# Layer 1's self-attention in a two-layer decoder: layernorms and output in halves, projections three units later, a copy written as a maximum, first shifts placed ahead of two maxima

## The chip, the cores and the metric

The kernel runs on one core of one Trainium2 chip. The metric is the device time of one execution in microseconds (us). A core has five engines that run side by side and meet through semaphores: TensorE (PE in the profile; its weight loads are PEld), VectorE (DVE), ScalarE (ACT), GpSimd (POOL) and SyncE (SP), which here only issues DMAs. Each engine takes its own instructions in order. PE writes its results to PSUM, from where VectorE or ScalarE fetch them; PSUM is handed out in banks of 128 partitions by 512 fp32 values.

## The reference, cut to what matters

Two decoder layers, each self-attention, cross-attention and a feed-forward part, with a residual sum and a layernorm behind each. `x` is 2 batches of 1024 tokens with 256 features. The change lies in the second layer's self-attention (16 heads of 16 features) and in the two layernorms around it: the one behind layer 0's feed-forward part and its own.

```python
def _layernorm(x, axis=-1, eps=1e-05):
    m = jnp.mean(x, axis=axis, keepdims=True)
    v = jnp.var(x, axis=axis, keepdims=True)
    return (x - m) / jnp.sqrt(v + eps)

def _L1_attn_ref(x, W_qkv, b_qkv, W_proj, b_proj):
    B, N, C = x.shape
    qkv = (x @ W_qkv + b_qkv).reshape(B, N, 3, NUM_HEADS, HEAD_DIM)
    q, k, v = jnp.transpose(qkv, (2, 0, 3, 1, 4))
    scores = jnp.einsum('bhqd,bhkd->bhqk', q, k) * SCALE
    attn = jax.nn.softmax(scores, axis=-1)
    out = jnp.einsum('bhqk,bhkd->bhqd', attn, v)
    out = jnp.transpose(out, (0, 2, 1, 3)).reshape(B, N, C)
    return out @ W_proj + b_proj
...
x = _layernorm(x + _L0_ffn_ref(x, ...), axis=-1)
x = _layernorm(x + _L1_attn_ref(x, L1_attn_W_qkv, ...), axis=-1)
```

## The kernel before

The 2048 tokens are four groups (`g`) of 512: groups 0 and 1 are batch 0, groups 2 and 3 batch 1. A group's activations are a tile `x[g]` of 128 partitions by 4 tiles of 256 features.

`l1_attn` (from L1098) works through 16 **steps** `n`: batch, four heads (a quad) and half of the query rows. A step has eight **units**, one for each 128 keys (`kt`), so unit `u` belongs to step `u // 8`, and the loop runs over 128 units. Of PE, VectorE and ScalarE the order of instructions is the order of this Python text (`manual_schedule`); POOL and SP are ordered by a scheduler. In each unit stand, in this order:

- every eighth unit (7, 15, 23, ...), `shifts(n)` for the next step: four small VectorE operations on 128x16 values. L1197 takes the minimum of two halves, L1199 rounds it to the fp32r format, L1200 copies it into the tile `cz`, and L1201 writes what the rounding left off. They turn the softmax's row maxima into rows that a matmul can add to the scores;
- `maxima` twice: each time two matmuls (L1177), each into a bank of its own, and two VectorE reductions (L1187) that take the row maxima out of those banks. They run nine units ahead of the scores that need them. The banks come from a pool of three (`ps_t`), which the projections, transposes and outputs share;
- between the two, `products`: eight matmuls for the scores (L1222) and for adding the shift (L1228), and two exponentials on ScalarE (L1234);
- in the shift units `shifted(n)`: PE transposes `cz` (L1208), and VectorE brings the result to SBUF as `c` (L70);
- `mix` of the unit before: probabilities times values into the accumulator (L1248);
- `others(unit)`: what a table `extra` holds for this unit. `at(unit, f, ...)` fills the table.

That table carries all the rest. `project` makes queries and keys of a batch: PE (L1086), a bias on ScalarE (L1091), the upper bits on VectorE (L1094), the remainder on POOL (L1095: `ql` and `kl`). `stacks` copies them by DMA on SP into `qst` and `kst`, the layout that the matmuls read. `values` makes the values (L1134, L1139). `taken` and `quotient` divide a finished step by its sums (L1268, L1272, L1273). For a group whose heads are all done, `turned` transposes the attention's result (L1286), `output` multiplies it by the output weights (L1301) and adds it to a residual sum `r` (L1306), `weigh` takes the layernorm's statistics, `normed` scales, and `onward` transposes the new `x` for the next stage (L157). The layernorms of groups 2 and 3 from layer 0 also lie in the table, at units 11 and 19; those of groups 0 and 1 were done before the loop.

`moments` (L170 to L184) takes four `bn_stats` and four `bn_aggr` in turn (L178, L179), adds epsilon (L181) and lets POOL raise to the power -0.5 (L183); `scaled` then makes four scalings on VectorE (L200). The residual sum `r` starts as `x` plus the bias on POOL (L1294) in one of four buffers `r`. For groups 0 and 1 this buffer is the one that held the sums of groups 2 and 3, so the addition waits until L200 has read those.

Ahead of the loop, nine early units (-9 to -1) fill the maxima of step 0 and the first two of step 1 (L1182, 128x1024 at a time), with the values and projections of batch 0 in between; then come `shifts(0)` and `shifted(0)`. What group 3 needs at the end (`self.ends`) is interleaved with the first four iterations of the cross-attention.

The table's entries before:

```python
for g, unit in ((2, 11), (3, 19)):
    for k, f in enumerate((weigh, normed, self.turned)):
        at(unit + k, f, g)
...
at(first - 26 + i, project, b, quad // 2, name, blk)
...
at(first - 20 + 2 * k + i, stacks, b, 2 * quad + k, name)
...
at(first - 22 + k, values, b, k)
...
for k, f in ((10, turned), (11, output), (13, normed), (15, onward)):
    at(first + k, f, g)
```

`first` is `8 * n`. In the loop, projections are made for step 8 (`first` = 64) and step 12 (`first` = 96), so at units 38 to 41 and 70 to 73.

Of the kernel before, what the change touches and what calls it, by code (L numbers as in the profile page):

```python
# [9 lines left out]
F32 = mybir.dt.float32  # L10
# [5 lines left out]
ALU = mybir.AluOpType  # L16
# [17 lines left out]
class Decoder:  # L34
# [136 lines left out]
    def moments(self, r, tiles):  # L171

        nc = self.nc
        n = len(tiles)
        mv = self.sm.tile([P, 4, 2], F32, tag="mv", name="mv")
        for k, i in enumerate(tiles):
            st = self.sm.tile([P, 6], F32, tag="st", name="st")
            nc.vector.bn_stats(st, r[:, i, :])  # L178
# [5 lines left out]
        return mv, rstd  # L184

    def scaled(self, x, r, tiles, mv, rstd, by=None):
        nc = self.nc
# [909 lines left out]
    def l1_attn(self):  # L1097
# [3 lines left out]
        with ExitStack() as s:  # L1101
# [60 lines left out]
            def maxima(u, early=False):  # L1162

                if u >= 16 * len(steps):
                    return
                n, k = u // 16, u % 16 // 8
                qt, kb = divmod(u % 8, 2)
                b, quad, qb = steps[n]
                jp = 2 * quad + k
                if u % 16 == 0:  # L1170
                    most[n] = self.sm.tile([P, 2, 4, 4], F32, tag="most", name="most")
                q0 = qb * 512 + qt * P
                both = self.wide() if early else None
                sc = [both[:, a, :] if early else self.bank() for a in range(2)]
                for a in range(2):
                    rows = slice(64 * a, 64 * a + 64)
                    nc.tensor.matmul(  # L1177
                        sc[a], lhsT=stack[b, jp, "q"][rows, q0 : q0 + P],
                        rhs=stack[b, jp, "k"][rows, kb * 512 : (kb + 1) * 512], start=True, stop=True,
                    )  # L1180
                if early:
                    nc.vector.tensor_reduce(  # L1182
                        most[n][:, kb, qt, k : k + 3 : 2], both, AX.X, ALU.max, negate=True
                    )
                for a in range(0 if early else 2):
                    h = 2 * a + k
                    nc.vector.tensor_reduce(  # L1187
                        most[n][:, kb, qt, h : h + 1], sc[a], AX.X, ALU.max, negate=True
                    )

            def shifts(n):

                if n >= len(steps):
                    return
                cz = zeros[n % 2]
                nm = self.sm.tile([P, 4, 4], F32, tag="nm8", name="nm8")
                nc.vector.tensor_tensor(nm, most[n][:, 0], most[n][:, 1], ALU.min)  # L1197
                hi = self.sm.tile([P, 4, 4], F32R, tag="nmh", name="nmh")
                nc.vector.tensor_copy(hi, nm)  # L1199
                nc.vector.tensor_copy(cz[:, :, :, 0], hi.bitcast(F32))  # L1200
                nc.vector.tensor_tensor(cz[:, :, :, 1], nm, hi.bitcast(F32), ALU.subtract)  # L1201

            def shifted(n):
# [88 lines left out]
            def output(g):  # L1292
                r = self.rp.tile([P, 4, D], F32, tag="r", name="r")
                nc.gpsimd.tensor_tensor(  # L1294
                    r, self.x[g], self.lbp.unsqueeze(1).to_broadcast([P, 4, D]), ALU.add
                )
                for i in range(0, 4, 2):
                    ps = self.bank().rearrange("p (i d) -> p i d", i=2)
                    for k in range(2):
                        for c in range(2):  # L1300
                            nc.tensor.matmul(  # L1301
                                ps[:, k, :], lhsT=aT[g][:, c, (i + k) * P : (i + k + 1) * P],
                                rhs=wo[:, c, :], start=c == 0, stop=c == 1,
                            )
                    rv = r[:, i : i + 2, :]
                    nc.vector.tensor_tensor(rv, ps, rv, ALU.add)  # L1306
                weigh(g, r)

            sums = {}

            def weigh(g, r=None):
                r = self.sums[g] if r is None else r
                sums[g] = r, self.moments(r, range(4))

            def normed(g):
                r, moments = sums.pop(g)
                self.x[g] = self.xp.tile([P, 4, D], F32, tag="x", name="xg")
                self.scaled(self.x[g], r, range(4), *moments)

            def onward(g):  # L1320
                nxT[g] = self.transposed(self.x[g])
# [4 lines left out]
            def at(unit, f, *args):  # L1326
                extra.setdefault(unit, []).append((f, args))

            for g, unit in ((2, 11), (3, 19)):
                for k, f in enumerate((weigh, normed, self.turned)):  # L1330
                    at(unit + k, f, g)
            last = 8 * len(steps)
            both = [(name, blk) for name in "qk" for blk in range(2)]
            for n, (b, quad, qb) in enumerate(steps):
                first = 8 * n
                if qb == 0:
                    for i, (name, blk) in enumerate(both):
                        if quad % 2 == 0 and n > 4:
                            at(first - 26 + i, project, b, quad // 2, name, blk)
                    for i, name in enumerate("qk" if n else ()):  # L1340
                        for k in range(2):
                            at(first - 20 + 2 * k + i, stacks, b, 2 * quad + k, name)
                    if quad == 0 and n:
                        for k in range(4):
                            at(first - 22 + k, values, b, k)
                at(first + 8, taken, n)
                at(first + 9, quotient, n)
                if quad == 3 and n < len(steps) - 1:
                    g = 2 * b + qb
                    for k, f in ((10, turned), (11, output), (13, normed), (15, onward)):  # L1350
                        at(first + k, f, g)

            def others(unit):
                for f, args in extra.pop(unit, ()):
# [498 lines left out]
```

## Time and profile before

| what | us |
|---|---|
| median of 3 runs (2458.32 to 2465.51) | 2461.87 |
| the profiled execution | 2461.69 |
| its span, first to last instruction | 2459.9 |
| PE busy (14062 matmul records) | 2345.8 |
| VectorE busy | 1680.9 |
| ScalarE busy | 1106.2 |
| POOL busy | 910.4 |
| row maxima L1187 in layer 1's self-attention, 476 instructions, 683 ns each | 296.3 |
| first early maximum to last product of layer 1's self-attention | 1770.7 to 2241 |

The page divides the span into 40 slices of 61.5 us. Each digit is the busy share of a slice in tenths, PEclk the granted TensorE clock:

```profile
PE   7999999999998999999999999999999999999974
...
DVE  6887887888785234555555555555689687995776
...
PEclk9999999999999999999999999999989999999986
```

The digits from the 30th to the 37th slice are layer 1's self-attention: PE is at nine tenths or more, VectorE mostly at 6 to 9. The clock dips in the 30th slice.

In the stage itself the waits show in full only when single instructions are read in order of time; the trace gives each one's start, its length, and how long its engine idled before it, with the instruction that released it.

### The profile page before, as it was taken

What the parts mean: (1) busy time and instruction counts of PE and PEld (TensorE: products, weight loads), DVE (VectorE), ACT (ScalarE), POOL (GpSimd) and SP (SyncE); (2) the same over time, 40 slices, a digit from 0 to 9 for tenths busy, and PEclk for the clock granted to TensorE, in tenths of its full rate; (3) what the DMA queues carried; (4) which work ended last, traced back from release to release, by engine and by line L of the source; (5) the groups of instructions that cost most, each with busy time, mean ns of one, the idle gap of its engine ahead of it and who ended that gap; (6) DMA issues with size and microseconds to landing.
All of it is one profiled execution on the core that took longest, in us unless ns stands there. A gap on an engine that the chain in (4) does not pass through costs nothing.

```text
span 2459.9 us, 37289 instructions
## 1 busy us (share of the span) xinstructions
PE 2345.8 (95%) x14062; PEld 1599.9 (65%) x14065; DVE 1680.9 (68%) x2924; ACT 1106.2 (45%) x1722; POOL 910.4 (37%) x748
## 2 busy tenths in 40 slices
PE   7999999999998999999999999999999999999974
PEld 3545545545545668899999999999844444555742
DVE  6887887888785234555555555555689687995776
ACT  5665565565563322333333233333256554664344
POOL 4666566566565222342242433332210001002412
PEclk9999999999999999999999999999989999999986
DMA  7888788688787001010010010100212122210001
GB/s 158 174 159 168 149 169 169 131 163 171 148 172 187 1 0 41 1 39 27 13 35 25 23 35 12 48 1 1 47 28 40 30 37 34 44 27 1 1 1 35
DMA packets 275667, 168.78 MB, mean 69 GB/s; under 512 B 47560, under 2 KB 262176, under 8 KB 275488
## 3 DMA queue, kind: packets, MB, share of 16 engines
q1 hardware_dynamic: 239072, 148.05, 28.8%
q10 hardware_dynamic: 36416, 18.36, 3.7%
q8 instruction: 111, 1.82, 0.3%
q14 instruction: 68, 0.56, 0.1%
HBM read 34.21 MB, written 2.10 MB: 15 GB/s over the span
## 4 chain that ended last, share of the span: by engine, by line
PE 73%; DVE 12%; DMA 4%; SPq 3%; issue 3%; ACT 3%; POOL 1%; ACTq 0%; DVEq 0%; POOLq 0%
PE unit L917 16%; PE acc L965 9%; PE bank L965 7%; PE wide L297 6%; PE acc L1248 5%; PE acc L379 4%; PE bank L1177 3%; SPq L358 3%; PE bank L252 3%; DMA turned<-blocks 3%; PE wide L649 2%; DVE most L1187 2%; PE bank L662 2%; DVE blocks L342 2%; PE wide L1222 2%
## 5 line engine op out<-in xcount | busy, mean ns | idle before, releaser
L312 DVE TENSOR_REDUCE nm<-wide 128x1 f32<-128x1024 f32 x256 | 300.9, 1215 | 62.9 <-PE wide L297 61.9
L1187 DVE TENSOR_REDUCE most<-bank 128x1 f32<-128x512 f32 x476 | 296.3, 683 | 23.7 <-PE bank L1177 23.3
L1234 ACT ACTIVATE w<-wide 128x1024 f32<-128x1024 f32 x256 | 248.2, 1022 | 140.9 <-PE wide L1228 132.0
L297 PE MATMUL wide<-k,q 64*128 64x512 f32 x1024 | 274.0, 632 | 18.0 <-ACT p L317 16.6
L328 POOL TENSOR_SCALAR p<-p,sums 128x1024 f32<-128x1024 f32 x128 | 143.1, 1118 | 270.6 <-DVE sums L325 270.6
L379 PE MATMUL acc<-turned,v 128*64 128x256 f32 x2048 | 235.1, 382 | 2.2 <-ACT aoT L74 1.3
L379 PEld LDWEIGHTS acc<-turned,v 128*64 128x64 f32 x2048 | 142.6, 137 | 114.3 <-issue 34.8
L906 ACT ACTIVATE mhT<-mhT,cols 128x256 f32<-128x256 f32 (+1 forms) x256 | 143.3, 607 | 147.4 <-DVE mhT L934 104.9
L317 ACT ACTIVATE p<-wide,nm 128x1024 f32<-128x1024 f32 x128 | 142.8, 1116 | 144.9 <-DVE nm L312 118.6
L817 POOL TENSOR_TENSOR hs<-hs,mhT 128x1024 f32<-128x1024 f32 x31 | 102.4, 3305 | 241.8 <-DVE hs L815 241.8
L342 DVE STREAM_TRANSPOSE blocks<-p 128x1024 f32<-128x1024 f32 x128 | 158.1, 1235 | 45.9 <-DMA turned<-blocks 19.8
L297 PEld LDWEIGHTS wide<-k,q 64*128 64x128 f32 x1024 | 90.4, 187 | 145.3 <-issue 74.5
L917 PE MATMUL unit<-xT,w 128*128 128x256 f32 x768 | 182.2, 379 | 0.0
L183 POOL TENSOR_TENSOR rstd<-ve,nhalf 128x4 f32<-128x4 f32 (+2 forms) x28 | 26.1, 932 | 421.4 <-DVE ve L181 421.0
L974 DVE SCALAR_TENSOR_TENSOR r<-acc,gates,r 128x128 f32<-128x128 f32 x256 | 77.8, 346 | 140.0 <-PE acc L965 140.0
L342 DVE STREAM_TRANSPOSE blocks<-r 128x1024 f32<-128x1024 f32 x128 | 153.9, 1203 | 0.0
L1177 PE MATMUL bank<-kst,qst 64*128 64x512 f32 x476 | 139.1, 480 | 14.8 <-DVE most L1187 14.5
L917 PEld LDWEIGHTS unit<-xT,w 128*128 128x128 f32 x768 | 140.9, 190 | 16.9 <-issue 0.3
L1177 PEld LDWEIGHTS bank<-kst,qst 64*128 64x128 f32 x476 | 67.5, 188 | 127.1 <-DVE most L1187 105.1
L328 POOL TENSOR_SCALAR r<-r,sums 128x1024 f32<-128x1024 f32 x128 | 143.2, 1119 | 0.0
L317 ACT ACTIVATE r<-wide,nm 128x1024 f32<-128x1024 f32 x128 | 142.3, 1111 | 1.0 <-DVE nm L312 0.7
L1248 PE MATMUL acc<-w,v 128*32 128x512 f32 x1024 | 140.5, 621 | 0.0
(332 smaller groups left out, 4604.7 us busy)
## 6 DMA issues: line engine op xcount, KB each, us to landing
turned<-blocks SPq DMA_DIRECT2D x636, 128.0 KB, 2.8
turned<-blocks ACTq DMA_DIRECT2D x132, 128.0 KB, 3.2
w<-in_L_ffn_W SPq DMA_DIRECT2D x16, 1024.0 KB, 5.2
q<-q SPq DMA_DIRECT2D x64, 128.0 KB, 2.3
k<-k SPq DMA_DIRECT2D x32, 128.0 KB, 2.7
qst<-qh SPq DMA_DIRECT2D x48, 64.0 KB, 2.4
qst<-ql SPq DMA_DIRECT2D x48, 64.0 KB, 2.4
kst<-kh SPq DMA_DIRECT2D x48, 64.0 KB
```

What stands on the lines that cost most here:

```text
L297: nc.tensor.matmul(sc[h][:, kb, :], lhsT=q[rows, qi, at : at + P], rhs=k[rows, ki, :], start=True, stop=True,)
L312: nc.vector.tensor_reduce(nm, sc, AX.XY, ALU.max, negate=True)
L317: nc.scalar.activation(p, sc.rearrange("p a c -> p (a c)"), AF.Exp, bias=nm, accum_out=sums[:, 0, h : h + 1],)
L328: nc.gpsimd.tensor_scalar(p, p, sums[:, 1, h : h + 1], 1.0, ALU.mult, ALU.mult)
L342: nc.vector.transpose(blocks[m][:, :, h, qt, :], p.rearrange("p (j q) -> p j q", q=32))
L379: nc.tensor.matmul(av[own[h], 0:256].rearrange("p (t i q) -> p i t q", t=2, i=4), lhsT=vals[u][:, kt, own[h]], rhs=p[:, h], start=kt == 0, ...
L917: nc.tensor.matmul(v[:, m, :], lhsT=up[e][k][:, f : f + P], rhs=self.halves[g][k], start=k in (1, 2, 5) and m == 0, stop=True, skip_group_ ...
L965: nc.tensor.matmul(ps[at][:, m * P : (m + 1) * P], lhsT=h[k][:, c, m * P : (m + 1) * P], rhs=down[e][k][:, c, :], start=k in (1, 2, 5) and ...
L1177: nc.tensor.matmul(sc[a], lhsT=stack[b, jp, "q"][rows, q0 : q0 + P], rhs=stack[b, jp, "k"][rows, kb * 512 : (kb + 1) * 512], start=True, s ...
L1187: nc.vector.tensor_reduce(most[n][:, kb, qt, h : h + 1], sc[a], AX.X, ALU.max, negate=True)
L1234: nc.scalar.activation(slot[:, k, :], ps[k].rearrange("p a q -> p (a q)"), AF.Exp, scale=0.25)
L1248: nc.tensor.matmul(mixed[n][o : o + 32, :], lhsT=vals[b][:, kt, 17 * h : 17 * h + 32], rhs=pT[:, a, :], start=kt == 0, stop=kt == 7, tile_ ...
```

## The change

The layernorm gets a second form in halves. `weighed` takes the statistics of two tiles (two `bn_stats`, then two `bn_aggr`), with epsilon and the power behind the second half; `scaled_half` scales two tiles. `output` is split in two halves, with its residual addition on POOL in a function of its own, `residual`. The table is refilled accordingly, so that the pieces stand in units of their own and the chain of a group ends two units later. All of `project`, `stacks` and `values` move three units later. In `shifts` the second copy is written as a maximum over an axis of length one. `shifts(0)` moves ahead of the maxima of unit -1. A function `turned_half` is added that nothing calls (left out below).

```diff
--- before.py
+++ after.py
@@ -182,6 +182,37 @@
         rstd = self.sm.tile([P, 4], F32, tag="rstd", name="rstd")
         nc.gpsimd.tensor_tensor(rstd[:, 0:n], ve[:, 0:n], self.nhalf[:, 0:n], ALU.pow)
         return mv, rstd
+
+    def weighed(self, r, mv=None):
+
+        nc = self.nc
+        tiles = (0, 1) if mv is None else (2, 3)
+        if mv is None:
+            mv = self.sm.tile([P, 4, 2], F32, tag="mv", name="mv")
+        st = [self.sm.tile([P, 6], F32, tag="st", name="st") for _ in tiles]
+        for k, i in enumerate(tiles):
+            nc.vector.bn_stats(st[k], r[:, i, :])
+        for k, i in enumerate(tiles):
+            nc.vector.bn_aggr(mv[:, i, :], st[k])
+        if tiles[0] == 0:
+            return mv
+        ve = self.sm.tile([P, 4], F32, tag="ve", name="ve")
+        nc.vector.tensor_scalar(ve, mv[:, :, 1], EPS, None, ALU.add)
+        rstd = self.sm.tile([P, 4], F32, tag="rstd", name="rstd")
+        nc.gpsimd.tensor_tensor(rstd, ve, self.nhalf, ALU.pow)
+        return mv, rstd
+
+    def scaled_half(self, x, r, half, mv, rstd):
+        i = slice(2 * half, 2 * half + 2)
+        self.scaled(x, r, range(2 * half, 2 * half + 2), mv[:, i, :], rstd[:, i])
+
...
 
     def scaled(self, x, r, tiles, mv, rstd, by=None):
         nc = self.nc
@@ -1197,7 +1228,10 @@
                 nc.vector.tensor_tensor(nm, most[n][:, 0], most[n][:, 1], ALU.min)
                 hi = self.sm.tile([P, 4, 4], F32R, tag="nmh", name="nmh")
                 nc.vector.tensor_copy(hi, nm)
-                nc.vector.tensor_copy(cz[:, :, :, 0], hi.bitcast(F32))
+
+                nc.vector.tensor_reduce(
+                    cz[:, :, :, 0], hi.bitcast(F32).unsqueeze(3), AX.X, ALU.max
+                )
                 nc.vector.tensor_tensor(cz[:, :, :, 1], nm, hi.bitcast(F32), ALU.subtract)
 
             def shifted(n):
@@ -1289,33 +1323,42 @@
                         )
                     self.evac(aT[g][:, c, :], ps)
 
-            def output(g):
-                r = self.rp.tile([P, 4, D], F32, tag="r", name="r")
+            sums = {}
+
+            def residual(g):
+                r = sums[g] = self.rp.tile([P, 4, D], F32, tag="r", name="r")
                 nc.gpsimd.tensor_tensor(
                     r, self.x[g], self.lbp.unsqueeze(1).to_broadcast([P, 4, D]), ALU.add
                 )
-                for i in range(0, 4, 2):
-                    ps = self.bank().rearrange("p (i d) -> p i d", i=2)
-                    for k in range(2):
-                        for c in range(2):
-                            nc.tensor.matmul(
-                                ps[:, k, :], lhsT=aT[g][:, c, (i + k) * P : (i + k + 1) * P],
-                                rhs=wo[:, c, :], start=c == 0, stop=c == 1,
-                            )
-                    rv = r[:, i : i + 2, :]
-                    nc.vector.tensor_tensor(rv, ps, rv, ALU.add)
-                weigh(g, r)
-
-            sums = {}
-
-            def weigh(g, r=None):
-                r = self.sums[g] if r is None else r
-                sums[g] = r, self.moments(r, range(4))
-
-            def normed(g):
-                r, moments = sums.pop(g)
-                self.x[g] = self.xp.tile([P, 4, D], F32, tag="x", name="xg")
-                self.scaled(self.x[g], r, range(4), *moments)
+
+            def output(g, half):
+                ps = self.bank().rearrange("p (i d) -> p i d", i=2)
+                for k in range(2):
+                    for c in range(2):
+                        i = 2 * half + k
+                        nc.tensor.matmul(
+                            ps[:, k, :], lhsT=aT[g][:, c, i * P : (i + 1) * P],
+                            rhs=wo[:, c, :], start=c == 0, stop=c == 1,
+                        )
+                rv = sums[g][:, 2 * half : 2 * half + 2, :]
+                nc.vector.tensor_tensor(rv, ps, rv, ALU.add)
+
+            moments = {}
+
+            def weigh(g, half):
+                if half == 0:
+                    sums.setdefault(g, self.sums[g])
+                moments[g] = self.weighed(sums[g], moments.get(g))
+
+            def normed(g, half):
+                if half == 0:
+                    new[g] = self.xp.tile([P, 4, D], F32, tag="x", name="xg")
+                self.scaled_half(new[g], sums[g], half, *moments[g])
+                if half:
+                    self.x[g] = new.pop(g)
+                    del sums[g], moments[g]
+
+            new = {}
 
             def onward(g):
                 nxT[g] = self.transposed(self.x[g])
@@ -1327,8 +1370,10 @@
                 extra.setdefault(unit, []).append((f, args))
 
             for g, unit in ((2, 11), (3, 19)):
-                for k, f in enumerate((weigh, normed, self.turned)):
-                    at(unit + k, f, g)
+                for k, f in enumerate((weigh, normed)):
+                    for half in range(2):
+                        at(unit + 2 * k + half, f, g, half)
+                at(unit + 4, self.turned, g)
             last = 8 * len(steps)
             both = [(name, blk) for name in "qk" for blk in range(2)]
             for n, (b, quad, qb) in enumerate(steps):
@@ -1336,19 +1381,23 @@
                 if qb == 0:
                     for i, (name, blk) in enumerate(both):
                         if quad % 2 == 0 and n > 4:
-                            at(first - 26 + i, project, b, quad // 2, name, blk)
+                            at(first - 23 + i, project, b, quad // 2, name, blk)
                     for i, name in enumerate("qk" if n else ()):
                         for k in range(2):
-                            at(first - 20 + 2 * k + i, stacks, b, 2 * quad + k, name)
+                            at(first - 17 + 2 * k + i, stacks, b, 2 * quad + k, name)
                     if quad == 0 and n:
                         for k in range(4):
-                            at(first - 22 + k, values, b, k)
+                            at(first - 19 + k, values, b, k)
                 at(first + 8, taken, n)
                 at(first + 9, quotient, n)
                 if quad == 3 and n < len(steps) - 1:
                     g = 2 * b + qb
-                    for k, f in ((10, turned), (11, output), (13, normed), (15, onward)):
-                        at(first + k, f, g)
+                    at(first + 10, residual, g)
+                    at(first + 10, turned, g)
+                    for k, f in ((11, output), (13, weigh), (15, normed)):
+                        for half in range(2):
+                            at(first + k + half, f, g, half)
+                    at(first + 17, onward, g)
 
             def others(unit):
                 for f, args in extra.pop(unit, ()):
@@ -1362,12 +1411,13 @@
                 jobs = [lambda k=k: values(0, k) for k in range(4)]
                 jobs += [lambda a=a: project(0, 1, *a) for a in both]
                 for unit in range(-9, 0):
+                    if unit == -1:
+                        shifts(0)
                     maxima(2 * unit + 18, True)
                     maxima(2 * unit + 19, True)
                     if jobs:
                         jobs.pop(0)()
                     others(unit)
-                shifts(0)
                 shifted(0)
                 late = None
                 for unit in range(last + 1):
@@ -1386,7 +1436,11 @@
                     others(unit)
                 for unit in sorted(extra):
                     others(unit)
-            self.ends = [lambda f=f: f(3) for f in (turned, output, normed, onward)]
+            both = lambda f: [f(3, half) for half in range(2)]
+            self.ends = [
+                lambda: (residual(3), turned(3)), lambda: (both(output), both(weigh)),
+                lambda: both(normed), lambda: onward(3),
+            ]
             self.xT = nxT
```

More of the change, by code (lines that the diff above doesn't have):

```diff
@@ L184, in moments, with turned_half @@
         return mv, rstd
+    def weighed(self, r, mv=None):
[18 more added lines that the diff above has]
+        self.scaled(x, r, range(2 * half, 2 * half + 2), mv[:, i, :], rstd[:, i])
+    def turned_half(self, xT, xg, c):
+        ps = self.bank()
+        for i in range(4):
+            self.nc.tensor.transpose(
+                ps[:, i * P : (i + 1) * P], xg[:, i, c * P : (c + 1) * P], self.ident
+            )
+        self.evac(xT[:, c, :], ps, by=self.nc.scalar)
     def scaled(self, x, r, tiles, mv, rstd, by=None):
@@ L1296, in output @@
                 )
-                for i in range(0, 4, 2):
-                    ps = self.bank().rearrange("p (i d) -> p i d", i=2)
-                    for k in range(2):
-                        for c in range(2):
-                            nc.tensor.matmul(
-                                ps[:, k, :], lhsT=aT[g][:, c, (i + k) * P : (i + k + 1) * P],
-                                rhs=wo[:, c, :], start=c == 0, stop=c == 1,
-                            )
-                    rv = r[:, i : i + 2, :]
-                    nc.vector.tensor_tensor(rv, ps, rv, ALU.add)
-                weigh(g, r)
-            sums = {}
-            def weigh(g, r=None):
-                r = self.sums[g] if r is None else r
-                sums[g] = r, self.moments(r, range(4))
-            def normed(g):
-                r, moments = sums.pop(g)
-                self.x[g] = self.xp.tile([P, 4, D], F32, tag="x", name="xg")
-                self.scaled(self.x[g], r, range(4), *moments)
+            def output(g, half):
[6 more added lines that the diff above has]
+                            rhs=wo[:, c, :], start=c == 0, stop=c == 1,
+                        )
+                rv = sums[g][:, 2 * half : 2 * half + 2, :]
[13 more added lines that the diff above has]
+            new = {}
             def onward(g):
```

## The prediction

> **What bounds the kernel now.** I went from the page to the stretch that the diff touches. The page's busy shares (PE 95%) say only that TensorE is the bound on average. A table of busy time by 40 us stretch, from 1760 to 2280 us, shows that layer 1's self-attention is not uniform. Its columns are the stretch, its length, busy time of PE, PEld, DVE, ACT and POOL (with counts), granted TensorE clock, DMA share, GB/s:
> ```profile
> 2040.00:2080.00 40.00, 35.05 (x187) 17.47 (x187) 25.63 (x53) 16.82 (x21) 3.56 (x3) 0.91 0.16 26
> ...
> 2160.00:2200.00 40.00, 39.75 (x286) 19.95 (x286) 36.63 (x68) 27.43 (x30) 0.00 (x0) 1.00 0.15 24
> ```
> The second row is the undisturbed loop: PE full, VectorE 92% busy, full clock. The first has idle PE and a clock of 0.91. The waits of this stretch say who is late (waiter, releaser, us in total, times, longest):
> ```profile
> PEld bank L1177 <- DVE most L1187: 105.1, 130, 2.6
> ...
> PE bank L1177 <- DVE most L1187: 14.5, 15, 2.1
> ```
> The maxima's matmuls wait for a PSUM bank that a VectorE reduction has yet to read. The first row costs little, for weight loads run ahead; the second is PE idle. So what counts is whatever sits in front of L1187 in VectorE's queue.
>
> To price it I read the chain of waits, where each step's first mixing matmul after a shift stands (start, us, what):
> ```profile
> 1824.49 0.99 PE acc L1248 x8
> ...
> 1852.85 0.99 PE acc L1248 x8
> ...
> 1881.12 1.00 PE acc L1248 x8
> ...
> 1904.69 0.99 PE acc L1248 x8
> ```
> An undisturbed step of eight units takes 1904.69 - 1881.12 = 23.57 us (eight times 2.70, quotient 0.59, shift transposes 0.56, and 0.82 lost at the shift). Subtracting that and the PE work of the extras (1.02 for eight transposes, 1.92 for a projection or a values part, 3.65 for an output) from every step leaves the **loss**:
> - steps 1 and 2 (layernorms of groups 2 and 3): 28.36 and 28.33 us, less 23.57 and 1.02: 3.8 each;
> - steps 4 and 5 (1904.7 to 1932.5 to 1973.0; first projections at units 38 to 41): 2.3 and 3.5;
> - step 7 (to 2029.8; layernorm of group 0): 5.0;
> - steps 8 and 9 (to 2068.8 and 2101.5; layernorm of group 1, last projections): 7.8 and 2.3.
>
> 28.5 us in all is what can be won in the loop; later steps lose nothing.
>
> **How a layernorm loses.** VectorE and PE in order of time (start, us; brackets: idle before, releaser):
> ```profile
> 1837.24 0.42 DVE L178 BATCH_NORM_STATS2 st<-r 128x6 f32<-128x256 f32 x1
> ...
> 1839.57 2.48 DVE L1187 TENSOR_REDUCE most<-bank 128x1 f32<-128x512 f32 x4
> 1841.97 1.38 DVE L200 TENSOR_SCALAR xg<-r,mv,rstd 128x256 f32<-128x256 f32 x4
> ```
> ```profile
> 1840.31 0.50 PE L1177 MATMUL bank<-kst,qst 64*128 64x512 f32 x1 [1.64 <-DVE most L1187]
> ```
> The statistics hold VectorE for 1839.57 - 1837.24 = 2.33 us, and the unit takes 4.72 us instead of 2.70: 2.02 lost, so about 0.31 is absorbed. Then the clock, in half-microsecond stretches:
> ```profile
> 1841.00:1841.50 0.50, 0.50 (x8) 0.00 (x0) 0.50 (x2) 0.00 (x0) 0.00 (x0) 1.00 0.00 0
> ...
> 1842.00:1842.50 0.50, 0.50 (x4) 0.39 (x4) 0.50 (x3) 0.00 (x0) 0.00 (x0) 0.50 0.00 0
> ```
> It is 0.50 for 3.4 us, which takes another 1.7 us; the scaling (1.29) hides under that. 2.02 + 1.7 is the 3.8 of the step. Six such half-clock windows lie between 1840 and 2071 us, each after 1.64 us or more of idle PE. The Trainium skill, "TensorE: Matmul & The Clock Gate", section "Why this matters for your kernels", asks only that idle gaps stay under some 3 us. By that rule the gaps here cost just themselves and the six windows (10 us) could not be won; the trace says a gap of 1.64 is enough, while 1.46 us of idle (at 2256) is not. I use the trace: splitting a stall of 2 us in two wins the clock too.
>
> **The change, part by part.**
>
> *Layernorms in halves.* Two statistics then two aggregates: by the rows of L178 and L179 some 0.86 us, the second half 1.07 with L181; scaling in two times 0.65. No work is removed beyond about 0.3 us. Absorbed are 0.31 once and 0.21 in each later unit (2.70 less the 2.49 that four reductions take). Loss (0.86 - 0.31) + (1.07 - 0.21) + 2 x (0.65 - 0.21) = 2.3, and 0.5 more because one of the units is a shift unit, which has no slack: **2.8 per layernorm**, no single gap reaching 1.64, so no clock window. The output's halves bring 1.83 us of PE work for 0.6 of VectorE and cost nothing. The tile x arrives two units later; its transposes follow directly, and the next user of xT is tens of units away.
>
> *What the later end collides with.* POOL's residual add waits for exactly this layernorm, since its buffer r is the one that the scaling reads:
> ```profile
> L1294 POOL TENSOR_TENSOR r<-xg,lbp x4: 2370/2388/2397, 1843.4 to 2089.3; 128x1024 f32<-128x1024 f32 x4
> ...
>   DVE xg L200: 5.3, 2
> ```
> Before, it ran beside maxima out of PSUM. Now, for groups 2 and 3, the second scaling ends at units 14 and 22, and the very next VectorE instructions are a shift (units 15 and 23): minimum, rounding, the new maximum, the subtraction L1201. The add (2.4 us) starts with them.
>
> *The copy as a maximum.* What it is aimed at:
> ```profile
> 1928.68 0.17 DVE L1199 CAST nmh<-nm 128x16 fp32r<-128x16 f32 x1
> 1928.89 1.13 DVE L1200 COPY cz<-nmh 128x16 f32<-128x16 f32 x1
> 1929.93 0.17 DVE L1201 TENSOR_TENSOR cz<-nm,nmh 128x16 f32<-128x16 f32 x1
> ```
> ```profile
> 1928.69 1.29 POOL L1095 TENSOR_TENSOR ql<-w,qh 128x512 f32<-128x512 f32 x1 [54.51 <-DVE nm L1197]
> ```
> The copy ends when POOL's subtraction ends; alone it takes 0.18. A reduction out of SBUF does not wait so: L1588 takes 1.21 us with or without POOL. But L1201, 0.1 us behind it, has two inputs in SBUF. The row nearest to it, with POOL's beside it:
> ```profile
> 1000.10 0.85 DVE L793 TENSOR_TENSOR esq<-emean,esq 128x64 f32<-128x64 f32 x1
> ```
> ```profile
> 998.53 2.34 POOL L818 TENSOR_TENSOR hs<-mhT,hs 128x1024 f32<-128x1024 f32 x1
> ```
> That small subtraction, 0.22 us when POOL rests, ended 0.08 after POOL did. The Trainium skill, "SBUF — State Buffer", section "SBUF: two separate sides", says why: the port pair that VectorE shares with GpSimd is an exclusive lock, taken by two-port copies and also by any VectorE operation with two SBUF inputs against a GpSimd one that reads SBUF. This rule speaks against the edit: the wait moves one instruction on. By the copy's row alone the edit would save 2 us at units 15 and 23; by rule and L793's row nothing. Ends: 0 and 2.0 each; I take the wait, **2.0**, as L793 is the same kind of operation. With it the gap passes 1.64 and the clock window returns, 1.7. Groups 2 and 3 then cost 2.8 + 2.0 + 1.7 = 6.5 each against 3.8: **+5.4**. (POOL's L183 starts ahead of the shifts of units 63 and 71 likewise. Its pow of 1.0 us is taken at 0: L815 ran 1.22 us, its usual time, inside a 10.5 us pow at 992 us. Other end: 0.6 each.)
>
> *Projections three units later.* Before, two of them meet the shifts of units 39 and 71: the 1.04 us of the copy's wait, gaps of 1.85 twice, two clock windows. Now they fall on units 41 to 44 and 73 to 76, with no shift among them. Each still loses 0.67 (a unit of 5.30 where 2.70 + 1.92 is due, VectorE waiting for ACT's bias): 2.7 per four. First four: 2.7 against 2.3 + 3.5, **-3.1**. Their SP transfers (stacks) keep their order and start no later: they wait for a stack buffer whose last reader is the product of unit 47, 63 or 79 (the first at 2027.63, in unit 63). The values parts move alike and lost nothing. One collision is made: POOL's two remaining adds follow the last projection back to back (2086.98, 4.74 us), ending 9.2 us after that projection starts; three units later that is about 0.9 us into the shift of unit 79.
>
> *Group 0's layernorm*: 2.8 against 5.0, **-2.2**. *Group 1's with the last projections*: 2.8 + 2.7 + 0.9 = 6.4 against 7.8 + 2.3, **-3.7**.
>
> *First shifts ahead of two maxima.* PE idles 3.23 us for L1201 at 1798.46, VectorE being busy with two maxima of 1.13 each. Now the subtraction waits for POOL's kl instead (to about 1796.8), then the maxima, then the copy c at 1799.1 instead of 1799.6: **-0.4**; ends -1.5 and +0.5.
>
> *End.* The last transposes now lie between the final mixing and its quotient and cover the 0.71 us wait at 2244.90: **-0.7**.
>
> Sum: +5.4 - 3.1 - 2.2 - 3.7 - 0.4 - 0.7 = **-4.7**. The profiled execution took 2461.69 us (span 2459.9), which is the median 2461.87 but for 0.2. Forecast **2457**, no change that can be told: I count 0.3%, 7.4 us, as the least that a measurement of this kernel separates. Its own range is 2451 to 2463.
>
> **Rivals.** (1) *The subtraction does not wait.* If 16 elements slip past the add, both 2.0 and 1.7 us go at units 15 and 23 and 0.9 at 79: -8.3 more, **2449**, faster. For it: no row of L1201 itself shows it under a POOL add. Against: L793, and L815 and L816, which stretch from 1.22 to 1.8 and 2.2 us under POOL. (2) *The clock halves earlier than I read.* The gaps now come in series, about 0.5 to 1.1 us in neighbouring windows. If 1.0 us of idle in a window is enough, groups 0 and 1 get a window each, groups 2 and 3 a second one, unit 79 one: five times 1.7, +8.5, **2465.5**, slower than before. For it: one window at 794 us halved after 1.2. Against: 1.28 at 1641 and 1.46 at 2256 did not. (3) *The projections' move alone counts*: the layernorm pieces give back all they win in collisions (unit 63's pow at its other end too): about **2460**.
>
> **Numbers.** Forecast 0.52, rival 1 0.23, rival 2 0.15, rival 3 0.10. Range 2446 to 2468, from rival 1 less 3 to rival 2 plus 2.5. Faster: rival 1 and the low tail of the forecast, 0.35; slower: the upper half of rival 2 and some of the rest, 0.11; within 0.3%: 0.54.
>
> **What will show it.** The subtraction behind the new maximum at about 2 us in two places; the maximum at 0.2 everywhere; half-clock windows after the shifts of units 15 and 23 but none around units 39, 60 and 71; steps 7 and 8 some 2 to 5 us shorter. A subtraction of 0.18 throughout would make rival 1 right; half clock in step 7 or 8, rival 2. A late stack, with maxima waiting for a DMA, would break the whole sum.

## The result and the profile after

Median 2459.32 us for the changed kernel (14 runs, 2452.33 to 2464.45) against 2460.27 for the kernel before (14 runs, 2452.39 to 2466.11). The ratio is 0.9992, with a 95% interval of [0.998, 1.0005], or between 4.9 us gained and 1.2 lost: no change that can be told.

The profiled execution took 2461.05 us (span 2459.3). Its page, busy tenths in 40 slices and the granted clock:

```profile
PE   7999999999998999999999999999998999999974
...
DVE  6887888887785334555565655555688777895786
...
PEclk9999999999999999999999999999999999999986
```

The dip of the clock in the 30th slice is gone; the two half-clock stretches that are left in this stage (below) fall into the next slice, too short to show in tenths. The table of busy time by stretch says the same (stretch, length, busy PE, PEld, DVE, ACT, POOL, clock, DMA share, GB/s):

```profile
2040.00:2080.00 40.00, 38.43 (x246) 20.39 (x246) 32.52 (x67) 22.09 (x25) 2.26 (x2) 1.00 0.22 35
2160.00:2200.00 40.00, 39.76 (x292) 20.57 (x292) 36.62 (x68) 26.49 (x29) 0.00 (x0) 1.00 0.17 27
```

The stretch that had 35.05 us of busy PE at a clock of 0.91 now has 38.43 at 1.00. But the waits (waiter, releaser, total, times, longest) hardly fell, and the longest grew from 2.1 to 2.7:

```profile
PE bank L1208 <- DVE most L1218: 12.9, 21, 2.7
```

L1208 and L1218 are the maxima's matmul and reduction, L1177 and L1187 before. Likewise the rounding is now L1230 (L1199), the copy, now a maximum, L1232 (L1200), the subtraction L1235 (L1201), the mixing L1282 (L1248), the residual add on POOL L1330 (L1294).

**Where the time went.** I measure the stage from its first early maximum to the transposes of its last quotient. It took 474.84 us before (1770.72 to 2245.55) and 470.72 after (1776.26 to 2246.99): 4.12 less. Yet it began 5.54 us later, with nothing edited ahead of it, and what follows it (where only the last group's output and layernorm come in halves) was 2.07 shorter; so the two spans differ by 0.6 only. Over all nine profiled executions of this study the stage begins between 1765.58 and 1776.26 and the rest takes 211.65 to 214.98 us, in an order that follows no edit: this is what a single run scatters by, and the stage's length is the steadier measure.

The chain of waits of the changed kernel shows the first steps (start, us, what; the rows are the first mixing after each shift):

```profile
1830.13 0.99 PE acc L1282 x8
...
1858.15 1.87 PE acc L1282 x8
...
1888.78 1.86 PE acc L1282 x8
...
1914.98 0.99 PE acc L1282 x8
```

The first two steps take 28.0 and 30.6 us and the third, undisturbed before, 26.2; the mixing lasts 1.87 instead of 0.99, being at half clock. All steps, from PE's rows:

| part of the stage | before | after | change | forecast |
|---|---|---|---|---|
| to the second shift's mix | 53.70 | 53.80 | +0.1 | -0.4 |
| steps 1 to 3 (layernorms of groups 2, 3) | 80.20 | 84.86 | +4.7 | +5.4 |
| steps 4 to 6 (first four projections) | 91.87 | 89.52 | -2.4 | -3.1 |
| step 7 (layernorm of group 0) | 33.24 | 30.61 | -2.6 | -2.2 |
| steps 8 and 9 (group 1, last projections) | 71.68 | 67.91 | -3.8 | -3.7 |
| the other steps | 144.15 | 144.02 | -0.1 | -0.7 |

Half-clock time can be counted apart: 1.7 us lost in each window of 3.4. Behind the start there were six such windows, now there are two. So the clock gave 6.8 us, and everything else lost 2.7. (The half clock at the start, 5.1 us lost, is the same in both.)

**Where the new stall lies.** VectorE at the shift of unit 15, and POOL beside it:

```profile
1852.62 0.72 DVE L231 TENSOR_SCALAR xg<-r,mv,rstd 128x256 f32<-128x256 f32 x2
1853.27 0.17 DVE L1228 TENSOR_TENSOR nm<-most 128x16 f32<-128x16 f32 x1
1853.47 2.35 DVE L1230 CAST nmh<-nm 128x16 fp32r<-128x16 f32 x1
1855.85 0.18 DVE L1232 TENSOR_REDUCE cz<-nmh 128x16 f32<-128x16 f32 x1
1855.93 0.17 DVE L1235 TENSOR_TENSOR cz<-nm,nmh 128x16 f32<-128x16 f32 x1
```
```profile
1853.42 2.35 POOL L1330 TENSOR_TENSOR r<-xg,lbp 128x1024 f32<-128x1024 f32 x1 [5.05 <-DVE nm L1228]
```
```profile
1856.75 0.50 PE L1208 MATMUL bank<-kst,qst 64*128 64x512 f32 x1 [2.70 <-DVE most L1218]
```

The scaling's end (1853.34) releases POOL's add, 0.08 us later. The row's bracket names the minimum, which ended at about the same moment; in a kernel below, where no minimum is near, the add follows the scaling by the same 0.08. The add starts some 0.04 us ahead of the rounding; the rounding of 16 elements a partition then lasts as long as the add, and PE idles 2.70 us. The clock by half microseconds, before and inside the window that follows:

```profile
1857.00:1857.50 0.50, 0.40 (x2) 0.15 (x2) 0.50 (x2) 0.00 (x0) 0.00 (x0) 1.00 0.41 74
...
1860.50:1861.00 0.50, 0.50 (x4) 0.50 (x3) 0.00 (x0) 0.00 (x0) 0.00 (x0) 0.50 0.64 98
```

Unit 23 repeats it (rounding 2.35 us at 1884.14, PE idle 2.70). The wait is at the shift where the forecast put it and near its size (2.2 us for 2.0), but one instruction earlier: on the rounding, not the subtraction. The experiments had to show that the subtraction would wait if it came first.

### The profile page after: what moved, and what is told of

Same layout as the page of the kernel before. It is cut to its first block, busy times and chain, and to the rows that moved or that the text cites. A ratio compares the mean times of both kernels' runs of the same rounds, so it can differ in the third digit from the quotient of the medians.

```text
span 2459.3 us, 37292 instructions
## 1 busy us (share of the span) xinstructions
PE 2342.5 (95%) x14065; PEld 1597.9 (65%) x14065; DVE 1681.3 (68%) x2924; ACT 1106.1 (45%) x1722; POOL 911.0 (37%) x748
## 4 chain that ended last, share of the span: by engine, by line
PE 74%; DVE 12%; SPq 4%; DMA 3%; issue 3%; ACT 2%; POOL 1%; ACTq 1%; DVEq 0%; POOLq 0%
PE unit L948 16%; PE acc L996 9%; PE bank L996 7%; PE wide L328 6%; PE acc L410 5%; PE acc L1282 4%; SPq L389 3%; PE bank L1208 3%; DVE most L1218 3%; PE bank L283 3%; PE wide L680 2%; PE bank L693 2%; PE bank L427 2%; DVE nm L343 2%; DMA turned<-blocks 2%
## 5 line engine op out<-in xcount | busy, mean ns | idle before, releaser
L1218 DVE TENSOR_REDUCE most<-bank 128x1 f32<-128x512 f32 x476 | 295.2, 681 | 19.0 <-PE bank L1208 18.5
L1208 PE MATMUL bank<-kst,qst 64*128 64x512 f32 x476 | 139.7, 473 | 13.1 <-DVE most L1218 12.9
L1208 PEld LDWEIGHTS bank<-kst,qst 64*128 64x128 f32 x476 | 67.2, 185 | 126.1 <-DVE most L1218 104.6
L1282 PE MATMUL acc<-w,v 128*32 128x512 f32 x1024 | 139.4, 615 | 0.0
L393 POOL COPY turned<-blocks 32x1024 f32<-32x1024 f32 x128 | 131.8, 1030 | 4.0 <-DVE blocks L373 0.3
```

What stands on the lines that cost most here:

```text
L1208: nc.tensor.matmul(sc[a], lhsT=stack[b, jp, "q"][rows, q0 : q0 + P], rhs=stack[b, jp, "k"][rows, kb * 512 : (kb + 1) * 512], start=True, s ...
L1218: nc.vector.tensor_reduce(most[n][:, kb, qt, h : h + 1], sc[a], AX.X, ALU.max, negate=True)
L1282: nc.tensor.matmul(mixed[n][o : o + 32, :], lhsT=vals[b][:, kt, 17 * h : 17 * h + 32], rhs=pT[:, a, :], start=kt == 0, stop=kt == 7, tile_ ...
```

## The experiments

Each was compared with runs of the kernel before on its own chip: medians 2458.74 us for the first four (11 runs) and 2459.72 for the other three (9 runs). Where I ran a kernel once, I read the stage's length and its rows, not the total.

**The rounding as a maximum too.** In the changed kernel:

```diff
-                nc.vector.tensor_copy(hi, nm)
+                nc.vector.tensor_reduce(hi, nm.unsqueeze(3), AX.X, ALU.max)
```

> The changed kernel with the rounding in the shifts also written as a maximum over an axis of one, so that only the first (minimum) and the last (subtraction) of the four small operations can meet POOL at the shared port. The stage (first early maximum to last quotient transpose in the profile) is 474.8 us before and 470.7 after. Theory (an operation with two inputs in SBUF waits for POOL's add as a copy does): the 2.35 us that the rounding takes at units 15 and 23 move to the subtraction (about 2.0 to 2.2), the two half-clock windows stay, stage 470.7 within 1. Rival (only copies and roundings wait, the subtraction slips past): no small operation over 0.3 us at units 15 and 23, both half-clock windows gone, stage about 463.

2448.43 us in one run. VectorE and POOL at unit 15:

```profile
1841.34 0.17 DVE L1230 TENSOR_REDUCE nmh<-nm 128x16 fp32r<-128x16 f32 x1
1841.54 0.18 DVE L1232 TENSOR_REDUCE cz<-nmh 128x16 f32<-128x16 f32 x1
1841.63 2.07 DVE L1235 TENSOR_TENSOR cz<-nm,nmh 128x16 f32<-128x16 f32 x1
```
```profile
1841.30 2.36 POOL L1330 TENSOR_TENSOR r<-xg,lbp 128x1024 f32<-128x1024 f32 x1 [5.05 <-DVE nm L1228]
```

Both maxima pass under the running add in 0.17 and 0.18; the subtraction waits until 1843.70, 0.04 after POOL. The half clock follows both times (from 1845.05 and 1875.77). So reductions do not wait, the two-input subtraction does, and rival 1 falls. The stage took 468.82 us, outside the 470.7 within 1 that was expected. Of the 1.9 less than in the changed kernel, 1.45 lie ahead of step 1: one half-clock window less there, and a first shift held for 0.90 (on the subtraction) instead of 1.25 (on the rounding), two things that this run does not separate. Most of the rest lies at units 15 and 23, where PE idled 2.44 us instead of 2.70.

**The copy back.** In the changed kernel:

```diff
-                nc.vector.tensor_reduce(
-                    cz[:, :, :, 0], hi.bitcast(F32).unsqueeze(3), AX.X, ALU.max
-                )
+                nc.vector.tensor_copy(cz[:, :, :, 0], hi.bitcast(F32))
```

> The changed kernel with the maximum of one written as a copy again, all else as changed. Theory: the maximum is worth nothing here, for the rounding ahead of it takes the whole wait at units 15 and 23 and no other shift meets POOL at that instruction; the copy takes 0.18 us everywhere, stage 470.7 within 1. Rival (the maximum is what keeps POOL's adds or subtractions from stopping VectorE): the copy stretched to 1 us or more at some shift, stage longer by 1 to 4 us.

2456.35 us in one run, stage 468.88. The copy took 0.18 throughout, behind a rounding that took the wait:

```profile
1847.84 2.35 DVE L1230 CAST nmh<-nm 128x16 fp32r<-128x16 f32 x1
1850.22 0.18 DVE L1232 COPY cz<-nmh 128x16 f32<-128x16 f32 x1
1850.30 0.18 DVE L1233 TENSOR_TENSOR cz<-nm,nmh 128x16 f32<-128x16 f32 x1
```

So the maximum is worth nothing. That this stage is 1.84 shorter, again outside the range expected, has another cause. PE idled 2.71 us at both units, but the clock halved after the first only; the stalls, and the stretches just after each:

```profile
1851.13 0.50 PE L1208 MATMUL bank<-kst,qst 64*128 64x512 f32 x1 [2.71 <-DVE most L1218]
...
1881.52 0.50 PE L1208 MATMUL bank<-kst,qst 64*128 64x512 f32 x1 [2.71 <-DVE most L1218]
```

```profile
1853.00:1854.00 1.00, 1.00 (x6) 0.40 (x3) 0.46 (x1) 0.00 (x0) 0.00 (x0) 0.50 0.73 111
...
1883.00:1884.00 1.00, 1.00 (x11) 0.30 (x4) 0.86 (x2) 0.00 (x0) 0.00 (x0) 1.00 0.00 0
```

The half clock began at 1852.95. The half-clock stretches here last 3.41 us or a multiple of it, and those of one stage start whole multiples of 3.41 us apart, so I count in windows of that length. Counted on from 1852.95, a boundary lies near 1880.25, inside the second idle (1878.81 to 1881.52), which it cuts into some 1.44 and 1.27; with PE's other idle moments the second of these windows holds 1.37 us, and neither is enough. The window that ended at 1852.95 holds 1.6 of the first idle and, with PE's other idle moments, 1.69 in all. So the same stall may cost 1.7 us more or not, by where the windows happen to lie. Counted so behind step 0 in all nine kernels, each window at full clock with 1.64 us or more of idle PE was followed by half clock (the least is in the kernel before, to 1841.97), and none with 1.60 or less was (the most is in the kernel with the first shifts back, to 1882.87). Outside this stage that bound does not always hold: windows of 1.2 us (the kernel before, to 797.5) and 0.9 (the split kernel below, to 2258.6) were followed by half clock too.

**Pieces of groups 2 and 3 one unit earlier.** In the changed kernel:

```diff
-            for g, unit in ((2, 11), (3, 19)):
+            for g, unit in ((2, 10), (3, 18)):
```

> The changed kernel with the layernorm pieces of groups 2 and 3 one unit earlier (from units 10 and 18 instead of 11 and 19), so that POOL's add starts one unit ahead of the shift and runs beside the row maxima, which read PSUM. Theory (the collision of the add with the shift costs 2.2 us of VectorE and a half-clock window of 1.7 us, twice): rounding 0.17 to 0.3 us at units 15 and 23, no half-clock window between 1850 and 2250 us, stage 470.7 - 7.8 = 463 (461.5 to 464.5), the kernel about 0.3% faster than the changed one. Rival (the halves themselves cost, by more instructions in units without slack): stage 469 to 471, the same time as the changed kernel.

2448.22 us median (6 runs), ratio to before 0.9955 [0.9938, 0.9971]; stage 462.38, as expected, 8.3 less than the changed kernel. The interval lies wholly below the changed kernel's [0.998, 1.0005]. The same shift, and POOL's add:

```profile
1851.35 0.17 DVE L1228 TENSOR_TENSOR nm<-most 128x16 f32<-128x16 f32 x1
1851.55 0.17 DVE L1230 CAST nmh<-nm 128x16 fp32r<-128x16 f32 x1
...
1851.85 0.18 DVE L1235 TENSOR_TENSOR cz<-nm,nmh 128x16 f32<-128x16 f32 x1
```
```profile
1848.05 2.38 POOL L1330 TENSOR_TENSOR r<-xg,lbp 128x1024 f32<-128x1024 f32 x1 [5.05 <-DVE xg L231]
```

The add is as long and no work is gone; it merely ends at 1850.43, before the shift, beside maxima read from PSUM that it does not delay (four in 2.47 us, as always). Steps 1 to 3 take 26.48, 26.46 and 23.56, and no window of steps 1 to 15 is at half clock. This shows the collision with POOL as the cause of what the pieces gave back.

**Projections back.** In the changed kernel, `project`, `stacks` and `values` at their old units:

```diff
-                            at(first - 23 + i, project, b, quad // 2, name, blk)
+                            at(first - 26 + i, project, b, quad // 2, name, blk)
...
-                            at(first - 17 + 2 * k + i, stacks, b, 2 * quad + k, name)
+                            at(first - 20 + 2 * k + i, stacks, b, 2 * quad + k, name)
...
-                            at(first - 19 + k, values, b, k)
+                            at(first - 22 + k, values, b, k)
```

> The changed kernel with projections, stacks and values at the units of before (three earlier). At the shifts of units 39 and 71 the POOL subtraction then runs beside the small operations again. Theory (two inputs in SBUF wait too): the maximum takes 0.18 us there, but the subtraction L1235 behind it about 1.1 us; two PE gaps of about 1.8 us and two half-clock windows return, stage 474.3 (473 to 476). Rival (the subtraction does not wait): it takes 0.18 us, the gaps stay below 1 us, stage 470 to 472.

2454.7 us in one run; stage 471.70, below the expected 473 to 476. Here too only one of the stalls of units 15 and 23 halved the clock; against the copy-back kernel, which shares that, the old places cost 2.8. Both collisions are back, at units 39 and 71; unit 71, with POOL:

```profile
2060.20 0.17 DVE L1230 CAST nmh<-nm 128x16 fp32r<-128x16 f32 x1
2060.41 0.18 DVE L1232 TENSOR_REDUCE cz<-nmh 128x16 f32<-128x16 f32 x1
2060.49 1.04 DVE L1235 TENSOR_TENSOR cz<-nm,nmh 128x16 f32<-128x16 f32 x1
```
```profile
2060.22 1.28 POOL L1126 TENSOR_TENSOR ql<-w,qh 128x512 f32<-128x512 f32 x1 [0.89 <-DVE nm L1228]
```

The rounding got in 0.02 us ahead of POOL, the maximum passed, the subtraction waited until POOL's end. Unit 39 is the very place that the copy's row of 1.13 us came from: with a maximum there, the wait is 1.05 on the next instruction (1.04 at unit 71), and each time a half-clock window follows (from 1933.25 and 2062.96). In the copy-back kernel, which has the move without the maximum, nothing waits at these two units. What removed these waits is the move, not the maximum.

**The move alone.** The kernel before with the three lines that the last diff undoes.

> The kernel before with one part of the change: projections, stacks and values three units later. My theory: the steps of groups 2 and 3 stay 28.3 us each, the steps 4 to 6 shrink together from 91.87 to about 89.5, and the POOL adds run into the shift of unit 79 (copy or rounding near 1 us there). Group 1's steps 8 and 9 keep group 1's statistics in one piece: between 68 and 71.7. Stage 470 to 473, so that this part alone gives about as much as the whole change (470.72). Rival 3 (only this move counts) expects the same 470 to 473; if the move won nothing by itself, 474.8.

2453.39 us in one run; stage 471.01, within what both theories expected. Alone the move gives 3.83 us. Steps 4 to 6 take 89.55, as in the changed kernel; steps 8 and 9 70.56 against its 67.91, step 7 33.32 against 30.61. So the pieces win 2.7 us at each of groups 0 and 1, and lose 5.2 at groups 2 and 3 (84.86 against 79.70 here, where one stall of 1.65 us, cut by a window's boundary, kept full clock): about nothing together. The collision of unit 79 comes with the move; the minimum there waits for the second of POOL's two adds:

```profile
2092.51 0.94 DVE L1197 TENSOR_TENSOR nm<-most 128x16 f32<-128x16 f32 x1
```

**Projections split.** The earlier pieces, and each projection of the second batch in two parts: matmuls and ScalarE's bias two units earlier than in the change, the upper bits on VectorE (with POOL's remainder) one unit after them. Of its edit, the table's lines for the projections:

```diff
-                            at(first - 23 + i, project, b, quad // 2, name, blk)
+                            at(first - 25 + i, projected, b, quad // 2, name, blk)
+                            at(first - 24 + i, split, b, quad // 2, name, blk)
```

> Layernorm pieces of groups 2 and 3 one unit earlier, and besides each projection of the second batch has its matmuls two units earlier and its upper-bits operation on VectorE one unit after them, so that VectorE no longer waits for ScalarE's bias. My theory: the eight losses of 0.67 go (-5.4) and POOL's two adds end before the shift of unit 79 (-0.9): stage 456 to 457.5 against 462.38 with the earlier pieces alone, whole about 2442. If the loss of 0.67 was VectorE's extra instruction itself (about 0.3) rather than the wait for ScalarE, only half goes: 459 to 460.

2444.67 us median (5 runs), ratio to before 0.9937 [0.9923, 0.9951]; stage 455.34, 0.7 below the expected 456 to 457.5. An upper-bits instruction of the changed kernel (first row) and of this one:

```profile
2094.11 0.43 DVE L1125 TENSOR_SCALAR kh<-w 128x512 int32<-128x512 int32 x1 [2.49 <-ACT w L1122]
```
```profile
2074.85 0.41 DVE L1127 TENSOR_SCALAR kh<-w 128x512 int32<-128x512 int32 x1
...
2083.11 0.17 DVE L1241 TENSOR_TENSOR nm<-most 128x16 f32<-128x16 f32 x1
```
```profile
2076.59 4.73 POOL L1343 TENSOR_TENSOR r<-xg,lbp 128x1024 f32<-128x1024 f32 x2
```

VectorE no longer idles ahead of it for ScalarE. Step 5 falls from 38.08 to 35.36, or 0.68 for each of four projections, so the loss of 0.67 was the wait and not the added instruction. Step 9 falls by 4.01: four times 0.68, and of the other 1.3 some 0.8 is PE's wait at unit 79, gone since POOL's adds end at 2081.32, before that shift; the last 0.5 I can't place. This is the fastest version of the study; against the earlier pieces alone it was not measured side by side, and only the stage (455.34 against 462.38) orders the two.

**First shifts back** behind the last two maxima, in the changed kernel:

```diff
-                    if unit == -1:
-                        shifts(0)
...
+                shifts(0)
                 shifted(0)
```

> The changed kernel with the first shifts behind the last two maxima again. My theory: from the stage's start to the first mix 35.2 to 35.9 us, the same as with the edit (35.54), for the rounding waits for POOL's subtraction in the one order and the maxima stand ahead of it in the other. If the early shifts had won the 0.4 forecast, and something else took it back, this reads 35.9 to 36.4.

2458.99 us in one run. From the stage's start to the first mix it took 34.69, below the expected range and below the changed kernel's 35.54: a miss. The stage took 468.74, but the clock halved after one of its two stalls only, as in the copy-back kernel. Up to the end of step 0, two windows fewer were at half clock here (1.7 us lost instead of 5.1), to which I put it down without having tried it. Read on VectorE, from the last upper-bits operation to the copy c, VectorE took 4.35 us with the early shifts (1800.97 to 1805.32) and 4.63 without (1797.73 to 1802.36). Of the 0.4 forecast 0.28 is there, less than this place scatters by: to the first mix the three kernels without the early shifts take 34.69 to 35.36, the six with them 34.70 to 35.54. Whether it reaches the end I leave open.

## Why the prediction was right, and where its steps were off

*Bound and clock.* Right: what sits ahead of the maxima's reductions on VectorE set the changes of steps 1 to 9, and a stall of some 2 us can cost a half-clock window besides. The forecast windows came (after units 15 and 23) and went (none around units 39, 60 and 71), so rival 2 falls: idles of 0.98 us in the layernorms of groups 0 and 1 (1.08 and 0.98 in their windows) did not halve the clock. The Trainium skill, "TensorE: Matmul & The Clock Gate", section "Why this matters for your kernels", would have let gaps of up to some 3 us pass; two of 2.70 cost 1.7 each here. The same page calls the window free-running ("What's actually happening"); the copy-back kernel agrees, with equal stalls of 2.71 and half clock after only one. My sum took a window for each such stall; of the ten stalls at units 15 and 23 in the five kernels that have them (the changed one, the rounding and the copy edits, projections back, first shifts back), seven were followed by half clock. That both were in the profiled run of the changed kernel is luck of where its windows lay.

*Groups 2 and 3: +5.4, measured +4.7.* The wait was real and came from POOL's add, as said. Its place was not: I let the rounding pass and put it on the subtraction. The rule I used names copies too, and the rounding is one: the skill's "SBUF — State Buffer", section "Who interferes with whom", lists casts among the operations that can take the shared pair and says that reductions never contend; all three show here (2.35 on the cast, 0.17 to 0.18 on reductions, 2.07 on the subtraction). The size of the terms: in the earlier-pieces kernel the pieces cost 26.47 - 23.57 - 1.02 = 1.9 a step. There no piece falls ahead of a shift, so the 0.5 that I had put on this is not in it, and 2.3 stands against the 1.9. Moving them won 8.3 / 2 = 4.2 a step, for stall, window and these 0.5, which I had at 2.0 + 1.7 + 0.5. So the collision had its forecast size, and the pieces alone were 0.4 cheaper.

*The maximum: nothing.* Right, by three kernels: written as a copy it took 0.18 all the same, in its old place the wait moved on to the subtraction, and with the rounding as a reduction too it did likewise.

*Projections: -3.1 and the shared -3.7.* Right in mechanism: 2.4 and 3.8 measured. What the first lacks is not the projections' wait: in the split kernel, where that is gone, steps 4 to 6 still take 86.82 us, 0.7 more than the 3 x 23.57 + 8 x 1.92 = 86.1 of my count. The 0.9 for unit 79 came as a minimum of 0.96 instead of 0.17, and 0.80 of idle PE.

*Group 0: -2.2*, measured -2.6. *First shifts: -0.4*: 0.28 at the copy c, nothing at the end that can be told. *End: -0.7*: wrong. The transposes left the gap they had filled. Without them the last mixing waits for ScalarE's last exponentials, so PE's wait changed its place:

```profile
2242.83 2.70 PE L1282 MATMUL acc<-w,v 128*32 128x512 f32 x16
```

The sixteen matmuls take 2.70 us where before two groups of eight took 1.06 and 1.07; the last step is 27.34 instead of 27.43.

*The sum.* -4.7 forecast for the stage, -4.1 measured. That it came so near is in part luck: by the table the terms are off by +0.5, -0.7, +0.7, -0.4, -0.1 and +0.6, which nearly cancel. The medians show 0.95 of it. Their interval just admits 4.1, and more cannot be said: one execution of each kernel was profiled, and its half-clock windows alone move a stage by 1.7 us apiece. Rival 3 (the move alone counts) is near the truth in its arithmetic, since the pieces win and lose alike; its total is too near the forecast's to separate them.

## What to carry to other kernels

When work on the critical engine is cut into pieces and so ends later, look at what its end releases on other engines, and what the critical engine runs just then: here a 2.4 us add landed on a 0.2 us rounding, and one unit earlier won back 8.3 us. Rewriting one of several small instructions so that it can't wait only hands the wait to the next one that can; move the other engine's work instead. And an instruction that waits for a neighbour's fresh result (the upper bits behind ScalarE's bias) is worth issuing a unit later before it is worth making shorter.

## What the hardware showed

- Which of the three small instructions waited depended on starts 0.02 to 0.04 us apart: POOL ahead of the rounding held it (POOL's row at 1853.42, the rounding's at 1853.47); POOL behind it (2060.22 against 2060.20) let it pass and held the subtraction.
- Each wait ended within 0.1 us of POOL's end, though the waiting instruction had only 16 elements a partition (0.17 alone, 2.35 held).
- A 2.71 us idle of PE kept full clock where a window's boundary cut it into some 1.44 and 1.27 us, and cost 3.4 us at half clock where 1.6 of it lay in one window that held 1.69 us of idle in all.
